# The first batch by input chunks over all outputs, W0 as one tile, and four adds moved: a two-layer fp32 kernel on one core

## The chip, the core and the metric

The kernel runs on one core of a Trainium2 chip. The metric is the device time of one execution in microseconds; for several runs the median is given. A profile is one execution taken by the hardware profiler; its span is the time from the first to the last recorded work on the core.

## What is computed

For each of 8 batches, x is 256 tokens by 1024 features, fp32. In short (the reference's two functions, without the parts that only make inputs):

```python
sign = (2 * mask - 1)                       # mask: (8, 1024, 1024) of int32
x = x + (x @ W0.T + b0 + (x @ sign) * coeff[b])
A, Bm = lora_As[itok], lora_Bs[itok]        # rank 16, one adapter per batch
x = x + (x @ W1.T + b1 + ((x @ A) @ Bm) * 2.0)
```

The first layer has its own weight for every batch: W0 transposed, plus coeff times the sign matrix. So 4 MB of mask have to be read for each batch, and each has to be scaled and added to W0 before TensorE can use it. The second layer has one weight for all.

## The kernel before, in words

Two groups of four batches. In each group, first layer for the four, then second layer for all of them together. All data lie feature-major: partitions are features, tokens are columns.

**First layer, batches 0 to 3** (`first_layer`, L229 to 269). A batch's mask comes in 8 pieces: output half h (0, 1) outermost, input group g (0 to 3) within it; a piece is two input chunks of 128 by 512 outputs, 512 KB. `pieces` (L139) lists them for all batches, and k is a piece's number. For each piece:
- `load(k)` (L161) issues its DMAs on SP's queue: the mask, for batch 0 the matching W0 part (its own tile for each h and g, L167), for h = 0 the x of two input chunks (256 KB). For k below BY_CHUNK = 6 mask and W0 come in two halves, one input chunk each (256 KB); the first x too (128 KB halves). The mask tiles have three buffers.
- `build(k)` (L197) makes the weight: ScalarE's activation (L215) turns the mask into c(2m - 1), VectorE's add (L218) adds W0. In halves where the load was in halves.
- 8 matmuls (L243; a 128x128 weight against 256 tokens) add into two banks of PSUM for the half. Each fp32 matmul stands in the trace as two records of matmul and two of weight load.

Loads run four pieces ahead of the matmuls, builds two ahead. At the end of a half the banks are read: in batches 1 to 3 by ScalarE with the bias (L258); in batch 0 by VectorE with bias and x (L262), because the identity of "x +" isn't in W0 yet. It is added to W0's diagonal blocks (L205, eight adds of 128x128 by VectorE) when piece 8 is built, and is in all later weights.

**Order of work.** Each engine runs its own instructions one after the other, in the order that the framework's scheduler lays down at build time; that can move an instruction ahead of the place where the program wrote it. `tc.issue_after(i)` puts what is written inside it behind instruction i on i's engine. So the reads of batch 0 stand behind the add of the piece two further on (L254), and the sums that prepare the second layer's weights (`combine_weights`) behind the latest build (L833).

**First layer, batches 4 to 7** (`Seven`): each batch as seven products of quarter size with sums of weights and tokens made by VectorE (L295, L311, matmuls L357).

**Second layer** (`second_layer`, L582). The same scheme of seven products on two levels: `plan` (L748) names seven outer products, and `run` (L671) does each as seven inner ones of 8 records (L612). A product's banks are named X, Z and Y; `read` (L661) takes a bank into the output's quarter, by VectorE's add where something is to be added (L664). `add` (L745, one 128x512 add at L746) sums quarters. `beside` is a generator of extra VectorE work, one step of which is written after each of several inner products. The lower-right output quarter c22 gets two such sums, e5 and e1; before the change both are in `last_quarter` (L808), beside the seventh outer product (A22), whose end is `finish` (L723), and the quarter is then stored. `down` and `up` (L640, L621) are the adapter's two small products; `up` also gives c22 its first values, copied by ScalarE (L638) during the fifth outer product.

The kernel's start (L818 to 824): four loads, a one-element activation that makes ScalarE load its table, two builds. c_row, the batch coefficients, is loaded on ScalarE's queue first (L89); TensorE runs idle matmuls meanwhile (L99).

Of the kernel before, what the change touches and what calls it, by code (L numbers as in the profile page):

```python
# [21 lines left out]

# [2 lines left out]
def kernel(  # L25
# [11 lines left out]
    lora_b: bass.AP,  # L37
    outT: bass.AP,
):

# [91 lines left out]
    make_identity(nc, ident)  # L132


    x_sb, m_sb, weff, w0_sb, raw, weff_at = {}, {}, {}, {}, {}, {}
    anchors = {}
    halves_0 = [(h, g) for h in range(2) for g in range(NG)]
    seven_order = [(0, 0), (0, 1), (0, 2), (0, 3), (1, 2), (1, 0), (1, 3), (1, 1)]
    pieces = [(b, h, g) for b in range(B) for h, g in (seven_order if b in SEVEN else halves_0)]  # L139

    def pair(name):
        return qpool.tile([P, 2, CG, OQ], F32, tag="q", name=name)

    def chunks(k: int):

        return [slice(c, c + 1) for c in range(CG)] if k < BY_CHUNK else [slice(0, CG)]

    def chunk(a, c: int):

        flat = a.rearrange("p c f -> (p c f)")  # L150
        return flat.rearrange("(c p f) -> c p f", c=CG, p=P)[c]


    W1_ORDER = [
# [6 lines left out]
    def load(k: int):  # L161


        b, h, g = pieces[k]
        m_sb[k] = mpool.tile([P, CG, OH], I32, tag="m", name=f"m_{k}")
        if b == 0:
            w0_sb[h, g] = const.tile([P, CG, OH], F32, tag=f"w0{h}{g}", name=f"w0_{h}_{g}")  # L167
        if h == 0:
            x_sb[b, g] = xpool.tile([P, CG, T], F32, tag=f"x{g}", name=f"x_{b}_{g}")
        pairs = [(m_sb[k], mask[b, h, g])]  # L170
        if b == 0:
            pairs.append((w0_sb[h, g], w0T[h, g]))
        if h == 0:
            pairs.append((x_sb[b, g], xT[b, g]))
        if k < BY_CHUNK:

            for c in range(CG):
                for i, (t, a) in enumerate(pairs):
                    if i < 2 or k == 0:
                        nc.sync.dma_start(t[:, c], chunk(a, c))  # L180
                    elif c == 0:
                        nc.sync.dma_start(t, a)
        else:
            for t, a in pairs:
                nc.sync.dma_start(t, a)
        if k == NG:
            nc.sync.dma_start(b0_sb, b0)
        if k == 2 * NG:
            nc.sync.dma_start(itok_sb, itok)
        for n, (q, r) in enumerate(W1_ORDER):  # L190
            if k == 0 and r % 2 == 0:
                two = pair(f"w1_{q}_{r // 2}")
                raw[q, r], raw[q, r + 1] = two[:, 0], two[:, 1]
            if k == 2 * NG + 2 + 3 * n // 4:
                nc.sync.dma_start(raw[q, r], w1T[q, r])

    def build(k: int):  # L197

        b, h, g = pieces[k]
        if k == 2 * NG:  # L200

            for c in range(NC):
                j = c % TPH
                d = w0_sb[c // TPH, c // CG][:, c % CG, j * P : (j + 1) * P]
                nc.vector.tensor_add(d, d, ident)  # L205
        if b not in SEVEN or (h == 0 and g < 3):
            pool, tag = wpool, "w"
        elif g >= NG // 2:
            pool, tag = tpool, "T"
        else:  # L210
            pool, tag = qpool, "q"
        w = pool.tile([P, CG, OH], F32, tag=tag, name=f"w_{k}")
        m = m_sb.pop(k)
        for c in chunks(k):
            nc.scalar.activation(  # L215
                w[:, c], m[:, c], AF.Identity, bias=neg_c[:, b : b + 1], scale=two_c[:, b : b + 1]
            )
            weff_at[k] = nc.vector.tensor_add(w[:, c], w[:, c], w0_sb[h, g][:, c])  # L218
            anchors["weights"] = weff_at[k]
        weff[k] = w  # L220

# [4 lines left out]
    def bank(name):  # L226
        return psum.tile([P, 2, T], F32, tag="ps", name=name)

    def first_layer(b: int, h: int, y, beside):  # L229


        ps = [bank(f"ps1_{b}_{h}_{i}") for i in range(TPH // 2)]
        for g in range(NG):
            k = (b * 2 + h) * NG + g
            if k + LOADS_AHEAD < n_pieces:
                load(k + LOADS_AHEAD)
            if k + BUILDS_AHEAD < n_pieces and pieces[k + BUILDS_AHEAD][0] not in SEVEN:
                build(k + BUILDS_AHEAD)
            w = weff.pop(k)
            for c in range(CG):  # L240
                for j in range(TPH):
                    first = g == 0 and c == 0
                    nc.tensor.matmul(  # L243
                        ps[j // 2][:, j % 2, :],
                        lhsT=w[:, c, j * P : (j + 1) * P],
                        rhs=x_sb[b, g][:, c, :],

                        start=first and j % 2 == 0,
                        stop=g == NG - 1 and c == CG - 1,
                        skip_group_check=True,  # L250
                    )
            beside(k)

        with tc.issue_after(weff_at[k + BUILDS_AHEAD].ins) if b == 0 else nullcontext():  # L254
            for j in range(TPH):
                ot = h * TPH + j
                if b > 0:
                    nc.scalar.activation(  # L258
                        y[:, j, :], ps[j // 2][:, j % 2, :], AF.Identity, bias=b0_sb[:, ot : ot + 1]
                    )  # L260
                    continue
                nc.vector.scalar_tensor_tensor(  # L262
                    y[:, j, :],
                    ps[j // 2][:, j % 2, :],
                    b0_sb[:, ot : ot + 1],
                    x_sb[b, ot // CG][:, ot % CG, :],
                    ALU.add,
                    ALU.add,
                )
# [3 lines left out]
    class Seven:  # L273
# [102 lines left out]
        def add(self, i, v, ps):  # L376
            nc.vector.tensor_add(self.out(i, v), ps, self.out(i, v))
# [37 lines left out]
    def behind(what: str):  # L415
        return tc.issue_after(anchors[what].ins) if what in anchors else nullcontext()

    class Sevens:
# [163 lines left out]
    def second_layer(group: int, y, first, first_steps, second):  # L582
# [78 lines left out]
        def read(out, ps, other=None):  # L661
            if other is None:
                return nc.scalar.copy(out, ps)  # L663
            return nc.vector.tensor_add(out, ps, other)  # L664
# [80 lines left out]
        def add(o, x):  # L745
            nc.vector.tensor_add(o, o, x)  # L746
# [91 lines left out]
    for group in range(NGROUP):  # L838
        y = [
            [  # L840
                ypool.tile([P, TPH, T], F32, tag=f"y{i}{h}", name=f"y_{GB * group + i}_{h}")
                for h in range(2)
            ]
            for i in range(GB)
        ]
        first = Right(f"b11_{group}", [y[0][0], y[1][0]])
        second = Right(f"b21_{group}", [y[0][1], y[1][1]])
        first_steps = first.sums()

        def between(b):  # L850
            if b % GB == 2 and group:
                load_adapters(group, y[1][0][:, 0, :1])
            if b % GB == 3:
                next(first_steps)
                next(first_steps)

        sevens[group].run(y, between)
        for i in range(GB):
            if GB * group + i in SEVEN:
                continue  # L860
            between(GB * group + i)
            for h in range(2):
# [12 lines left out]

# [68 lines left out]
```

## Time and profile before

| what | value |
|---|---|
| runs of the kernel, median of 3 | 412.73 us (412.66, 412.73, 423.72) |
| the profiled execution | 411.8 us |
| its span | 410.0 us |
| granted TensorE clock | 0.999 |
| moved by DMA | 97.44 MB, mean 238 GB/s |

Rows of the page's groups and of the timeline read: start and duration (timeline), line, engine, operation, output <- inputs, shape, count, then in brackets the idle time of the engine before it and what ended it. PE is TensorE's matmul, PEld its weight load, DVE is VectorE, ACT ScalarE, POOL GpSimd, SP the queue that issues most loads; a q after a name is the engine's queue of instructions that issue DMAs or wait. In a table of stretches each engine has its busy time and count of instructions, in the order PE, PEld, DVE, ACT, POOL; then come the granted clock, the busy share of the 16 DMA engines and what they moved. A row of DMA issues ends with KB each and the time from issue to landing.

### The profile page before, as it was taken

What the parts mean: (1) busy time and instruction counts of PE and PEld (TensorE: products, weight loads), DVE (VectorE), ACT (ScalarE), POOL (GpSimd) and SP (SyncE); (2) the same over time, 40 slices, a digit from 0 to 9 for tenths busy, and PEclk for the clock granted to TensorE, in tenths of its full rate; (3) what the DMA queues carried; (4) which work ended last, traced back from release to release, by engine and by line L of the source; (5) the groups of instructions that cost most, each with busy time, mean ns of one, the idle gap of its engine ahead of it and who ended that gap; (6) DMA issues with size and microseconds to landing.
All of it is one profiled execution on the core that took longest, in us unless ns stands there. A gap on an engine that the chain in (4) does not pass through costs nothing.

```text
span 410.0 us, 6576 instructions
## 1 busy us (share of the span) xinstructions
PE 403.4 (98%) x2458; PEld 357.4 (87%) x2458; DVE 302.0 (74%) x430; ACT 137.1 (33%) x216; POOL 38.5 (9%) x77
## 2 busy tenths in 40 slices
PE   7999999999999999999999999999999999999996
PEld 5888888888877888877899999999998788888885
DVE  2467597995647658995989999999936365886593
ACT  3544534534344201133115748274221420102200
POOL 0000042566301001000000000400000000000000
PEclk9999999999999999999999999999999999999999
DMA  7999999999997576775895768763022247555662
GB/s 252 388 403 392 296 368 415 412 405 320 413 342 250 139 230 201 217 224 184 235 364 154 258 198 292 221 213 97 26 74 77 77 135 242 165 146 165 194 217 103
DMA packets 42626, 97.44 MB, mean 238 GB/s; under 512 B 5604, under 2 KB 6372, under 8 KB 42596
## 3 DMA queue, kind: packets, MB, share of 16 engines
q1 hardware_dynamic: 33698, 76.30, 56.6%
q0 software_dynamic: 4288, 12.61, 8.1%
q10 hardware_dynamic: 4610, 8.13, 5.2%
q8 instruction: 19, 0.31, 0.3%
q14 instruction: 11, 0.09, 0.1%
HBM read 77.09 MB, written 19.92 MB: 237 GB/s over the span
## 4 chain that ended last, share of the span: by engine, by line
PE 90%; DVE 7%; DMA 1%; issue 1%; ACT 0%; SPq 0%; ACTq 0%; DVEq 0%
PE ps L243 27%; PE X L612 20%; PE X L357 14%; PE Z L612 10%; PE Z L357 7%; PE Y L612 5%; PE Y L357 3%; PE G L629 2%; PE psh L644 2%; DVE e L664 2%; DVE c L746 1%; DMA m<-mask 1%; DVE T L603 1%; DVE c L664 1%; SPq L180 0%
## 5 line engine op out<-in xcount | busy, mean ns | idle before, releaser
L215 ACT ACTIVATE w<-m,neg_c,two_c 128x1024 f32<-128x1024 int32 (+1 forms) x70 | 81.2, 1168 | 106.6 <-DMA m<-mask 44.2
L243 PE MATMUL ps<-x,w 128*128 128x256 f32 x512 | 111.3, 380 | 0.7 <-DVE w L218 0.7
L243 PEld LDWEIGHTS ps<-x,w 128*128 128x128 f32 x512 | 97.2, 190 | 14.9 <-DVE w L218 1.8
L218 DVE TENSOR_TENSOR w<-w,w 128x1024 f32<-128x1024 f32 (+1 forms) x70 | 77.7, 1128 | 32.9 <-ACT w L215 32.9
L746 DVE TENSOR_TENSOR c<-c,e 128x512 f32<-128x512 f32 x48 | 32.0, 686 | 10.1 <-ACT c L638 9.7
L357 PE MATMUL X<-t,s 128*128 128x128 f32 x256 | 29.9, 275 | 0.0
L357 PEld LDWEIGHTS X<-t,s 128*128 128x128 f32 x256 | 29.2, 192 | 0.0
L638 ACT COPY c<-G 128x512 f32<-128x512 f32 x32 | 16.4, 600 | 37.6 <-PE G L629 34.2
L372 ACT ACTIVATE y<-X,b_sb 128x128 f32<-128x128 f32 x48 | 13.6, 365 | 40.0 <-PE X L357 40.0
L664 DVE TENSOR_TENSOR c<-X,c 128x512 f32<-128x512 f32 (+1 forms) x26 | 16.6, 646 | 13.4 <-PE X L612 13.4
L663 ACT COPY e<-X 128x512 f32<-128x512 f32 x16 | 9.4, 588 | 48.0 <-PE X L612 48.0
L612 PE MATMUL X<-T_t,l_S_s 128*128 128x256 f32 x96 | 22.8, 380 | 0.0
L612 PEld LDWEIGHTS X<-T_t,l_S_s 128*128 128x128 f32 x96 | 18.2, 190 | 2.7 <-DVE e L664 0.3
L295 DVE TENSOR_TENSOR s<-w,w 128x1024 f32<-128x1024 f32 x16 | 19.2, 1215 | 0.0
L612 PE MATMUL X<-b_t,l_A_s 128*128 128x256 f32 x64 | 15.5, 386 | 0.0
L357 PE MATMUL Z<-x,s 128*128 128x128 f32 x128 | 15.0, 276 | 0.0
L357 PE MATMUL Y<-x,w 128*128 128x128 f32 x128 | 14.9, 275 | 0.0
L357 PE MATMUL X<-t,w 128*128 128x128 f32 x128 | 14.9, 275 | 0.0
L357 PE MATMUL Z<-t,s 128*128 128x128 f32 x128 | 14.9, 275 | 0.0
L357 PE MATMUL X<-x,w 128*128 128x128 f32 x128 | 14.9, 275 | 0.0
L357 PEld LDWEIGHTS X<-x,w 128*128 128x128 f32 x128 | 14.7, 192 | 0.1
L357 PEld LDWEIGHTS Z<-x,s 128*128 128x128 f32 x128 | 14.6, 192 | 0.0
(123 smaller groups left out, 589.3 us busy)
## 6 DMA issues: line engine op xcount, KB each, us to landing
m<-mask SPq DMA_DIRECT2D x58, 512.0 KB, 6.0
l_S_s<-leaf_S_s SPq DMA_DIRECT2D x32, 256.0 KB, 2.7
x<-xT SPq DMA_DIRECT2D x31, 256.0 KB, 5.4
outT<-c ACTq DMA_DIRECT2D x30, 256.0 KB, 3.5
l_A_s<-leaf_A_s SPq DMA_DIRECT2D x24, 256.0 KB, 3.3
l_S_a<-leaf_S_a SPq DMA_DIRECT2D x24, 256.0 KB, 2.8
w<-w1T SPq DMA_DIRECT2D x16, 256.0 KB, 7.3
leaf_S_s<-S_s POOLq DMA_DIRECT2D x16, 256.0 KB, 7.3
```

Source lines behind the costliest of these rows:

```text
L215: nc.scalar.activation(w[:, c], m[:, c], AF.Identity, bias=neg_c[:, b : b + 1], scale=two_c[:, b : b + 1])
L218: weff_at[k] = nc.vector.tensor_add(w[:, c], w[:, c], w0_sb[h, g][:, c])
L243: nc.tensor.matmul(ps[j // 2][:, j % 2, :], lhsT=w[:, c, j * P : (j + 1) * P], rhs=x_sb[b, g][:, c, :],  start=first and j % 2 == 0, stop= ...
L295: anchors["weights"] = op(s, self.w[x, a], self.w[y, a])
L357: nc.tensor.matmul(ps[:, j, :], lhsT=w[:, c, j * P : (j + 1) * P], rhs=r, start=first and a == 0 and c == 0 and j == 0, stop=False, skip_g ...
L372: nc.scalar.activation(self.out(i, v)[:, j, :], ps[:, j, :], AF.Identity, bias=b0_sb[:, ot : ot + 1])
L612: nc.tensor.matmul(ps[:, j, :], lhsT=l[:, c, j * P : (j + 1) * P], rhs=r[:, c, :], start=first and c == 0 and j == 0, stop=False, skip_gro ...
L629: nc.tensor.matmul(ps[b][:, j, :], lhsT=lb_pad[rows, o : o + P], rhs=h_sb[rows, :], start=j == 0, stop=j == 1, skip_group_check=True,)
L638: nc.scalar.copy(dest[b // 2][u, b % 2], ps[b])
L663: return nc.scalar.copy(out, ps)
L664: return nc.vector.tensor_add(out, ps, other)
L746: nc.vector.tensor_add(o, o, x)
```

## The change

Four things are changed; nothing else is.
- Batch 0 is no longer done half by half. Its piece k is one input chunk (128 rows) over all 1024 outputs: 512 KB of mask, 512 KB of W0. Eight pieces again; x (two chunks) comes with every second one. The eight output blocks add into four banks at once, and all eight reads stand after the eighth piece, behind the add of piece 9. The first three pieces (BY_HALF = 3) are loaded and built in two halves of 512 outputs each.
- The first x chunk is issued on ScalarE's queue instead of SP's.
- W0 is one tile of 128 x 8 x 1024 instead of eight; batches 1 to 7 use the part of it that belongs to their piece. The eight identity adds stand behind the add of piece 7.
- In the second layer the adds of e5 into c22 move from the seventh outer product into the sixth, each behind the latest VectorE read there.

The host lays mask and W0 out to match. The diff, cut to its core:

```diff
-BY_CHUNK = 6
+BY_HALF = 3
...
+    w0_sb = const.tile([P, NC, D], F32, tag="w0", name="w0_sb")
...
+    pieces = [(0, None, c) for c in range(NC)]
+    pieces += [(b, h, g) for b in range(1, B) for h, g in (by_seven if b in SEVEN else by_half)]
...
+    def parts(k: int):
+
+        return [slice(i, i + 1) for i in range(2)] if k < BY_HALF else [slice(0, 2)]
...
+    def w0_of(k: int):
+        b, h, g = pieces[k]
+        if b == 0:
+            return w0_sb[:, g, :].rearrange("p (h o) -> p h o", h=2)
+        return w0_sb[:, g * CG : (g + 1) * CG, h * OH : (h + 1) * OH]
...
+        m_sb[k] = mpool.tile([P, 2, OH], I32, tag="m", name=f"m_{k}")
+        pairs = [(m_sb[k], mask[b, g if b == 0 else h * NG + g])]
         if b == 0:
...
+            pairs.append((w0_of(k), w0T[g]))
+        x_pair = g // CG if b == 0 and g % CG == 0 else g if h == 0 else None
+        if x_pair is not None:
+            x = x_sb[b, x_pair] = xpool.tile([P, CG, T], F32, tag=f"x{x_pair}", name=f"x_{b}_{x_pair}")
+        if k < BY_HALF:
+
+            for i in range(2):
+                for t, a in pairs:
+                    nc.sync.dma_start(t[:, i], part(a, i))
+                if k == 0 and i == 0:
+                    nc.scalar.dma_start(x[:, 0], part(xT[0, 0], 0))
+                elif k == 0:
+                    nc.sync.dma_start(x[:, 1], part(xT[0, 0], 1))
+                elif x_pair is not None and i == 0:
+                    nc.sync.dma_start(x, xT[b, x_pair])
         else:
             for t, a in pairs:
                 nc.sync.dma_start(t, a)
+            if x_pair is not None:
+                nc.sync.dma_start(x, xT[b, x_pair])
...
             for c in range(NC):
-                j = c % TPH
-                d = w0_sb[c // TPH, c // CG][:, c % CG, j * P : (j + 1) * P]
-                nc.vector.tensor_add(d, d, ident)
+                d = w0_sb[:, c, c * P : (c + 1) * P]
+                with tc.issue_after(weff_at[k - 1].ins):
+                    nc.vector.tensor_add(d, d, ident)
...
-        for c in chunks(k):
+        for i in parts(k):
             nc.scalar.activation(
-                w[:, c], m[:, c], AF.Identity, bias=neg_c[:, b : b + 1], scale=two_c[:, b : b + 1]
+                w[:, i], m[:, i], AF.Identity, bias=neg_c[:, b : b + 1], scale=two_c[:, b : b + 1]
             )
-            weff_at[k] = nc.vector.tensor_add(w[:, c], w[:, c], w0_sb[h, g][:, c])
+            weff_at[k] = nc.vector.tensor_add(w[:, i], w[:, i], w0_of(k)[:, i])
...
+    def first_batch(y, beside):
+
+        ps = [bank(f"ps1_0_{i}") for i in range(NC // 2)]
+        for c in range(NC):
+            load(c + LOADS_AHEAD)
+            build(c + BUILDS_AHEAD)
+            w = weff.pop(c)
+            for ot in range(NC):
+                h, j = divmod(ot, TPH)
+                nc.tensor.matmul(
+                    ps[ot // 2][:, ot % 2, :],
+                    lhsT=w[:, h, j * P : (j + 1) * P],
+                    rhs=x_sb[0, c // CG][:, c % CG, :],
+                    start=c == 0 and ot % 2 == 0,
+                    stop=c == NC - 1,
+                    skip_group_check=True,
+                )
+            beside(c)
+
+        with tc.issue_after(weff_at[NC - 1 + BUILDS_AHEAD].ins):
+            for ot in range(NC):
+                h, j = divmod(ot, TPH)
                 nc.vector.scalar_tensor_tensor(
...
-            return nc.vector.tensor_add(out, ps, other)
+            anchors["reads"] = nc.vector.tensor_add(out, ps, other)
+            return anchors["reads"]
...
-        run(5, "S3", right["S3"], e1, e1, then=lambda uv: add(c21[uv], e1[uv]))
+
+        def add_e5():
+
+            for uv in UV:
+                with behind("reads"):
+                    add(c22[uv], e5[uv])
+                yield
+
+        run(5, "S3", right["S3"], e1, e1, beside=add_e5(), then=lambda uv: add(c21[uv], e1[uv]))
 
         def last_quarter():
             for u, v in UV:
-                add(c22[u, v], e5[u, v])
                 add(c22[u, v], e1[u, v])
                 store(c22[u, v], 1, 1, u, v)
                 yield
```

More of the change, by code (lines that the diff above doesn't have):

```diff
@@ L132, with part @@
     make_identity(nc, ident)
-    x_sb, m_sb, weff, w0_sb, raw, weff_at = {}, {}, {}, {}, {}, {}
+    x_sb, m_sb, weff, raw, weff_at = {}, {}, {}, {}, {}
     anchors = {}
-    halves_0 = [(h, g) for h in range(2) for g in range(NG)]
-    seven_order = [(0, 0), (0, 1), (0, 2), (0, 3), (1, 2), (1, 0), (1, 3), (1, 1)]
-    pieces = [(b, h, g) for b in range(B) for h, g in (seven_order if b in SEVEN else halves_0)]
+    w0_sb = const.tile([P, NC, D], F32, tag="w0", name="w0_sb")
+    by_half = [(h, g) for h in range(2) for g in range(NG)]
+    by_seven = [(0, 0), (0, 1), (0, 2), (0, 3), (1, 2), (1, 0), (1, 3), (1, 1)]
+    pieces = [(0, None, c) for c in range(NC)]
+    pieces += [(b, h, g) for b in range(1, B) for h, g in (by_seven if b in SEVEN else by_half)]
     def pair(name):
         return qpool.tile([P, 2, CG, OQ], F32, tag="q", name=name)
[L144 to L151, printed above, removed]
+    def parts(k: int):
+        return [slice(i, i + 1) for i in range(2)] if k < BY_HALF else [slice(0, 2)]
+    def part(a, i: int):
+        flat = a.rearrange("p i f -> (p i f)")
+        return flat.rearrange("(i p f) -> i p f", i=2, p=P)[i]
+    def w0_of(k: int):
[3 more added lines that the diff above has]
+        return w0_sb[:, g * CG : (g + 1) * CG, h * OH : (h + 1) * OH]
     W1_ORDER = [
@@ L164, in load @@
         b, h, g = pieces[k]
-        m_sb[k] = mpool.tile([P, CG, OH], I32, tag="m", name=f"m_{k}")
+        m_sb[k] = mpool.tile([P, 2, OH], I32, tag="m", name=f"m_{k}")
+        pairs = [(m_sb[k], mask[b, g if b == 0 else h * NG + g])]
         if b == 0:
[L167 to L182, printed above, removed]
+            pairs.append((w0_of(k), w0T[g]))
[12 more added lines that the diff above has]
+                    nc.sync.dma_start(x, xT[b, x_pair])
         else:
@@ L252, in first_layer @@
             beside(k)
[L254 to L261, printed above, removed]
+        for j in range(TPH):
+            ot = h * TPH + j
+            nc.scalar.activation(
+                y[:, j, :], ps[j // 2][:, j % 2, :], AF.Identity, bias=b0_sb[:, ot : ot + 1]
+            )
[14 more added lines that the diff above has]
+                    skip_group_check=True,
+                )
+            beside(c)
+        with tc.issue_after(weff_at[NC - 1 + BUILDS_AHEAD].ins):
+            for ot in range(NC):
+                h, j = divmod(ot, TPH)
                 nc.vector.scalar_tensor_tensor(
-                    y[:, j, :],
-                    ps[j // 2][:, j % 2, :],
+                    y[h][:, j, :],
+                    ps[ot // 2][:, ot % 2, :],
                     b0_sb[:, ot : ot + 1],
-                    x_sb[b, ot // CG][:, ot % CG, :],
+                    x_sb[0, ot // CG][:, ot % CG, :],
                     ALU.add,
@@ L861 @@
             between(GB * group + i)
+            if group == 0 and i == 0:
+                first_batch(y[0], step)
+                continue
             for h in range(2):
@@ L903, in pieces @@
         a = a.reshape(*lead, NG, CG, P, D // OH, OH)
-        return laid(a.transpose(*range(n), n + 3, n, n + 2, n + 1, n + 4))
+        a = a.transpose(*range(n), n + 3, n, n + 2, n + 1, n + 4)
+        return laid(a).reshape(*lead, -1, P, CG, OH)
     As = np.asarray(L1_cond_lora_As)
@@ L912 @@
         "mask": pieces(np.asarray(mask_Bx4096x4096_ik1)),
-        "w0T": pieces(np.asarray(L0_cond_W).T),
+        "w0T": laid(np.asarray(L0_cond_W).T.reshape(D // P, P, 2, OH)),
         "b0": laid(np.asarray(L0_cond_b).reshape(D // P, P).T),
@@ L923, with by_part @@
     }
-    def by_chunk(a):
-        a[:] = np.moveaxis(a, -2, -3).reshape(a.shape)
-    for k in range(BY_CHUNK):
-        by_chunk(arrays["mask"][0, k // NG, k % NG])
-        by_chunk(arrays["w0T"][k // NG, k % NG])
-    by_chunk(arrays["xT"][0, 0])
+    def by_part(a):
+        a[:] = np.moveaxis(a, 1, 0).reshape(a.shape)
+    arrays["mask"][0] = np.asarray(mask_Bx4096x4096_ik1)[0].reshape(D // P, P, 2, OH)
+    for k in range(BY_HALF):
+        by_part(arrays["mask"][0, k])
+        by_part(arrays["w0T"][k])
+    by_part(arrays["xT"][0, 0])
     nc = bacc.Bacc("TRN2", target_bir_lowering=False, num_devices=1)
```

## The prediction

> **What bounds the kernel now.** I read the engine shares first, then the chain that ended last.
>
> ```profile
> span 410.0 us, 6576 instructions
> PE 403.4 (98%) x2458; PEld 357.4 (87%) x2458; DVE 302.0 (74%) x430; ACT 137.1 (33%) x216; POOL 38.5 (9%) x77
> PE 90%; DVE 7%; DMA 1%; issue 1%; ACT 0%; SPq 0%; ACTq 0%; DVEq 0%
> ```
>
> TensorE is the bound nearly everywhere. A change that leaves the matmuls alone can only win what TensorE loses at its start, at its end, or in a hole. The chain in order of time, its first and longest pieces:
>
> ```profile
> 2.25 4.70 DMA m<-mask
> 6.98 0.82 ACT w L215
> 7.82 0.70 DVE w L218
> 8.57 109.26 PE ps L243 x504
> ```
>
> From 8.57 to 117.83 us TensorE works through the first layer of group 0. Elsewhere the chain has 24 records of the same kind (L612) in 5.18 us, 0.216 us each; 504 x 0.216 = 108.9, so only 0.4 us of 109.26 is idle. What stands ahead of 8.57 is the second half of piece 0: its mask was issued at 2.25 us and landed 4.7 us later. The timeline shows the holes:
>
> ```profile
> 5.71 1.76 PEld L243 LDWEIGHTS ps<-x,w 128*128 128x128 f32 x8 [0.39 <-DVE w L218]
> 8.57 3.32 PEld L243 LDWEIGHTS ps<-x,w 128*128 128x128 f32 x16 [1.10 <-DVE w L218]
> 12.23 27.92 PEld L243 LDWEIGHTS ps<-x,w 128*128 128x128 f32 x130 [0.34 <-DVE w L218]
> ```
>
> One step (half a piece, 4 matmuls, 8 records) is 1.73 us of TensorE. Step 0 starts at 5.8, step 1 at 8.57, step 3 waits 0.2 to 0.3 more, and then nothing visible. So the most that a better start could give is TensorE running gapless from about 5.5: 5.5 + 64 x 1.73 = 116.2 against 117.83, **1.6 us**. At the end:
>
> ```profile
> 396.87 1.29 DVE L746 TENSOR_TENSOR c<-c,e 128x512 f32<-128x512 f32 x2
> 404.37 1.89 PE L612 MATMUL X<-T_t,l_A_a 128*128 128x256 f32 x8
> 406.30 0.76 DVE L664 TENSOR_TENSOR c<-X,c 128x256 f32<-128x256 f32 x2 [1.04 <-PE X L612]
> ```
>
> The last of the adds at L746 is over at 398.2 us, 8 us before the last matmul; the tail (two half reads and their stores, 3.7 us) has none in it.
>
> What feeds the start is the DMA, in these stretches (DMA share and GB/s are the last two columns):
>
> ```profile
> 3.00:3.50 0.50, 0.50 (x2) 0.47 (x3) 0.24 (x2) 0.00 (x0) 0.00 (x0) 1.00 1.05 401
> 4.00:4.50 0.50, 0.50 (x2) 0.38 (x2) 0.00 (x0) 0.50 (x1) 0.00 (x0) 1.00 0.38 117
> 4.50:5.00 0.50, 0.50 (x3) 0.35 (x2) 0.44 (x1) 0.03 (x1) 0.00 (x0) 1.00 0.97 215
> 10.00:11.00 1.00, 1.00 (x6) 0.89 (x5) 0.76 (x4) 0.36 (x1) 0.00 (x0) 1.00 1.04 399
> ```
>
> A trough at 4 us, where the 128 KB half of the first x passes (third in SP's queue), and from 10 us on about 390 GB/s until 40 us. In batch 0 TensorE and the DMA run level.
>
> **Part 1: batch 0 by single input chunks.** Matmul count and shapes stay: 64 matmuls of two records. What changes is the bytes each stretch of TensorE needs. Before, each of the first four pieces (3.46 us of TensorE) needs mask 512 KB, W0 512 KB, x 256 KB, 1280 KB in all; the last four need 1024 KB. After, each needs 1152 KB on the mean. The sum, 9216 KB, is the same. I place landings on a line drawn through the trace: m of step 3 (2304 KB in the queue's order) landed at 10.6, m of step 11 (6912 KB) at 22.9, where its activation stopped waiting: 375 KB per us.
>
> Steps 0 and 1. x's first half goes to ScalarE's queue right behind c_row (issue ends 1.39), 0.4 us earlier than on SP, and is now the second thing in flight. Today it is what step 0 waits for: issued 1.78, landed 3.8 later at 5.58, while w was ready at 5.25. Step 0 can start at 5.3 to 5.5. Price on ScalarE: one issue of 0.43 us ahead of the table load (1.42 to 1.85, ending at 3.1) and the warm-up activation (to 3.3); the first real one waits for its mask until 3.67, which hides it with 0.35 us to spare. The next mask half moves up from fourth to third in SP's queue: issued at 1.78 instead of 2.25.
>
> Here the Trainium skill speaks against a gain: "DMA: Bandwidth & Descriptors", section "Issuing engines are not separate DMA queues", says that all issuers share the same 16 DMA engines and that a second issuer saves only the sequencer's issue time. By that rule the mask half comes 0.47 us earlier (one issue slot of SP) and the queue behind it not at all. The row says that around 4 us the DMA engines stood at a share of 0.38, so there was room and a filled trough is worth more: at 390 GB/s instead of 117 and 215, 0.4 MB in that one microsecond against 0.17, some 0.6 us. I take 0.35 us for everything behind (between nothing and 0.6, since x itself still has to pass), and 0.5 for the mask half: landed 6.45, activation 0.81, add 0.69, hand-over 0.1: step 1 at about 8.0 instead of 8.57. Step 2 (m at 1536 KB, landed 8.57 today, less 0.35) is ready at 9.8; it started at 10.3. So far 0.5 us won.
>
> An earlier step 0 also meets a TensorE that is still slow: the six idle loads from 3.11 us take 2.21 us, 0.4 us from one to the next, those after 6.2 us 0.215. So its first loads run at half the rate and it gains less than its 0.3 us. That counts for nothing in the sum, since step 1 waits for its own data. Steps 3 to 5 (masks at 2048, 2560 and 3328 KB, less 0.35, and 1.6 us of activation, add and hand-over) are ready at 11.2, 12.5 and 14.6, wanted at 11.5, 13.3 and 15.0: no hole.
>
> **Piece 3, where it is given back.** Halves end after piece 2 (BY_HALF = 3), which is step 5; before, they went on to step 11. Piece 3 is now one mask and one W0 load of 512 KB, one activation of 1.24 us and one add of 1.23, and none of its 8 matmuls starts before all of it. In SP's order its mask ends at 4096 KB and its W0 at 4608 KB: by the line 15.4 and 16.7, less 0.35: 15.0 and 16.4. The activation is over at 16.3; the add runs 16.4 to 17.6; step 6 starts at **17.7**. TensorE would want it at 9.8 + 4 x 1.73 = 16.7, so a new hole of 1.0 us opens. Before, the same step started at 8.57 + 5 x 1.73 + 0.2 = 17.4; counted back from 117.83, 58 steps of 1.727 give 17.65 with the later small gaps in it. The net is 0 to +0.3; I take **+0.1 us**.
>
> How sure is the landing? The nearest rows are the first and the second whole piece of the kernel before, pieces 6 and 7. Piece 6 landed on the line (24.9). Piece 7 did not:
>
> ```profile
> m<-mask SPq DMA_DIRECT2D x1, 512.0 KB, 7.5
> 28.57 1.24 ACT L215 ACTIVATE w<-m,neg_c,two_c 128x1024 f32<-128x1024 int32 x1 [2.40 <-DMA m<-mask]
> ```
>
> Issued at 20.94, landed at 28.45, where the line has 27.6: 0.8 late. Piece 3 is a first whole piece, so I take none of the 0.8, but keep it for the range. Then pieces 4 and 5: W0 at 5632 and 6912 KB, 19.1 and 22.5, ready at 20.4 and 23.8, wanted at 21.2 and 24.6: slack 0.8, gone if they are 0.8 late. x of pieces 2, 4 and 6 (3072, 5888, 8192 KB) lands 1 to 2 us ahead of need. SP itself: the mask of piece 3 needs the buffer of piece 0, free when step 1's activation ends (about 7.3); everything behind waits in SP with it, but over 1.5 MB is then still in flight, 4 us of work.
>
> **W0 as one tile; VectorE at the end of batch 0.** For the later batches the operand becomes two rows of 512 apart in one tile; the trace has no add of that form with one strided operand, the nearest is the plain one, 1.23 us; between 0 and 10% more would be 0.1 us on an engine with slack, so 0. The eight identity adds (0.28 us each, L205), until now scattered from 10 to 31 us, now stand together behind the add of piece 7 (over at 31): 2.0 us, and behind them the add of piece 8: over at 34.4, wanted at 35.0. The eight reads of the banks (four took 1.66 us, so 3.3) stand together behind the add of piece 9: 35.6 to 38.9, and behind them the add of piece 10 ends at 40.1 where TensorE wants it at 41.9. Both hidden, with 0.6 and 1.8 us left: 0.
>
> **The e5 adds.** Four adds of 0.69 us per group move from the seventh product into the sixth, behind its reads. TensorE does not wait for VectorE from 383 us on, nor in group 0 from 188 to 212, and the total is the same: 0 us, with under 0.3 us either way if a read shifts by one add.
>
> **Sum.** +0.1 us at step 6, 0 elsewhere: span 410.1, the profiled execution 411.8 becomes 411.9; the runs' median stands 0.9 above that execution, so **412.8 us**.
>
> **Rivals.**
> A. Forecast: start won, piece 3 gives it back, 412.2 to 413.4. For it: both terms come out of rows. Chance 0.50.
> B. Faster: the filled trough brings forward the whole queue by 0.6 us or more and the 4 KB rows of whole pieces run at the 404 to 412 GB/s seen from 22 to 28 us: W0 of piece 3 at 15.9, step 6 at 17.1, 0.6 less than A; at most the 1.6 us above. About 411.8. Against: the line has no such slack elsewhere. Chance 0.23.
> C. Slower: the second and later whole loads lag as piece 7 did. Place: step 6 to step 10; price: 0.8 us in W0 of piece 3 puts step 6 at 18.5, 413.6; with piece 5 late too, 414.2. It decides from a W0 landing after 16.6. Chance 0.23.
> D. The one tile is taken as one thing: an add then waits for every W0 load already issued. Four pieces ahead are 4.5 MB, 11 us: 424. Against: mask tiles are already loaded in two halves, and the first activation ran at 3.71 while the second half landed at 6.95. Chance 0.03; 0.01 is left for gains nobody sees.
>
> The range 411.3 to 414.5 leaves out D and the edges of B and C, under 0.2. 2% is 8.3 us, about what these runs (412.66 to 423.72) can tell from no change; only D reaches it: faster 0.01, same 0.96, slower 0.03.
>
> **What would show it.** Right: step 1 near 8.0; a hole of about 1 us before the matmuls of piece 3, ended by the add at L218; the first L612 matmul at 117.9 plus or minus 0.6; the tail still 3.7. Wrong: no trough at 4 us but step 1 unchanged (part 1), no hole at piece 3 (B), holes at pieces 4 and 5 (C), a wait of TensorE on VectorE at 35 or 42 us.

## The result, and the profile after

The changed kernel takes **410.92 us** (median of 11 runs, 410.14 to 412.68); the kernel before, on the same chip, 412.73 (11 runs, 411.66 to 423.72; the one of 423.72 is a slow run, which the ratio leaves out). The ratio is 0.9954, with a 95% interval of 0.9934 to 0.9974: within 2%, and still faster, by 1.1 to 2.7 us. The prediction said 412.8, in 411.3 to 414.5: the time lies below that range. The profiled execution took 410.92 us too, with a span of 409.1 instead of 410.0.

The page's shares of the engines, and the shares of the chain that ended last:

```profile
span 409.1 us, 6555 instructions
PE 403.8 (99%) x2458; PEld 358.2 (88%) x2458; DVE 300.7 (74%) x427; ACT 136.0 (33%) x213; POOL 38.6 (9%) x77
PE 91%; DMA 5%; ACT 2%; SPq 1%; DVE 0%; issue 0%; DVEq 0%; ACTq 0%
```

The matmuls are the same 2458 records. What differs is what TensorE lost between them, and the chain hints at where: before, VectorE held 7% of it, now 0%; the DMA held 1% and now 5%. Something on VectorE left the critical path, and transfers of masks took its place, at the start and again from 267 to 277 us.

**The start.** The chain's first pieces (start, length, what):

```profile
3.20 4.59 DMA m<-mask
8.57 5.90 DMA m<-mask
17.13 17.53 PE ps L280 x80
34.66 83.13 PE ps L255 x384
```

Its timeline over the same stretch (start, busy time, engine, line, and in brackets the idle time ahead and what ended it):

```profile
5.50 11.06 PEld L280 LDWEIGHTS ps<-x,w 128*128 128x128 f32 x48 [0.18 <-DVE w L230]
15.85 1.23 DVE L230 TENSOR_TENSOR w<-w,w_sb 128x1024 f32<-128x1024 f32 x1 [1.77 <-ACT w L227]
17.13 17.13 PEld L280 LDWEIGHTS ps<-x,w 128*128 128x128 f32 x80 [0.57 <-DVE w L230]
```

And two of the half-microsecond stretches (the last two columns are the DMA share and GB/s):

```profile
4.00:4.50 0.50, 0.50 (x2) 0.38 (x2) 0.00 (x0) 0.50 (x1) 0.00 (x0) 1.00 1.02 252
4.50:5.00 0.50, 0.50 (x3) 0.35 (x2) 0.25 (x1) 0.13 (x1) 0.00 (x0) 1.00 0.97 295
```

The trough at 4 us is filled (117 GB/s before, 252 now). The second mask half had landed by 6.07 us, step 1's operand was ready at 7.60, and from 5.5 to 16.6 us there is no pause of TensorE worth a line. Then comes the new hole ahead of piece 3: its add starts at 15.85 and TensorE idles 0.57 us until 17.13. Batch 0 ends at 34.66 (34.70 before, counted back from 117.83 by the same 83.13), the first layer of group 0 at 117.80 (117.83 before). So in this execution the whole of part 1 came to **0.03 us**. TensorE's waits from 16.5 to 117 us (sum, count, longest) say where the rest went, first of the changed kernel:

```profile
PEld ps L280 <- DVE w L230: 0.6, 1, 0.6
PEld ps L255 <- DVE w L230: 0.4, 1, 0.4
```

The second one, at 90 us, is for the weight made from the first mask of batch 3. From 9 to 117 us the kernel before had one wait in all:

```profile
PEld ps L243 <- DVE w L218: 0.3, 1, 0.3
```

**Where the 0.9 us of span is.** Down to 182 us the two traces run side by side, 0.03 apart. Then they part, in the fifth of the outer products of group 0. The kernel before, its timeline there (a stretch that the prediction did not show):

```profile
181.41 2.05 ACT L638 COPY c<-G 128x512 f32<-128x512 f32 x4 [3.31 <-DVE c L664]
182.38 1.89 PE L612 MATMUL X<-T,l_S_a 128*128 128x256 f32 x8
183.00 1.29 DVE L746 TENSOR_TENSOR c<-c,e 128x512 f32<-128x512 f32 x2 [0.95 <-ACT c L638]
184.21 0.69 DVE L664 TENSOR_TENSOR c<-X,c 128x512 f32<-128x512 f32 x1
184.95 1.99 PE L612 MATMUL X<-b_t,l_S_a 128*128 128x256 f32 x8 [0.68 <-DVE c L664]
```

The third line holds two e5 adds. The program writes them in the seventh product; the scheduler had placed them here, in the fifth, ahead of a read of bank X. VectorE takes its instructions in order: it idled 0.95 us until ScalarE had copied from G what they add to, added for 1.29 us, and only then read the bank. TensorE's next X product adds into that bank, so it has to wait for the read: it stood idle for 0.68 us in the matmul record (1.08 us in its load), and the bracket names the read, [<-DVE c L664]. The same stretch of the changed kernel:

```profile
181.37 2.05 ACT L669 COPY c<-G 128x512 f32<-128x512 f32 x4 [3.31 <-DVE c L695]
182.55 0.69 DVE L695 TENSOR_TENSOR c<-X,c 128x512 f32<-128x512 f32 x1 [0.53 <-PE X L643]
184.07 1.89 PE L643 MATMUL X<-b_t,l_S_a 128*128 128x256 f32 x8
184.96 0.68 DVE L778 TENSOR_TENSOR c<-c,e 128x512 f32<-128x512 f32 x1
```

The read comes first, at 182.55 instead of 184.21, the product starts without a wait, and the add at L778 goes in later, where nobody waits for it. What follows (the second run of G matmuls) begins at 185.97 instead of 186.95: 0.98 us, of which 0.03 is the start's. The same place in group 1 gives 0.22. The chain has it, first of the kernel before, then of the changed one:

```profile
375.22 5.60 PE X L612 x24
374.68 5.38 PE X L643 x24
```

The books: 0.03 at the start, 0.95 and 0.22 here, and 0.45 lost between 265 and 284 us, where TensorE waited twice, 0.2 us each, for ScalarE's reads, which stood behind activations of late masks of batches 4 to 7: 0.75 of the 0.9. The tail is as long as it was but for 0.1 us (405.55, the start of the last half reads, to 409.1; before, 406.30 to 410.0). The waits at that place come and go with the execution: there are none in the trace of the kernel before, 0.2 us of them in e5_alone, 1.1 in half8 and 1.4 in after_light, three of the runs below.

### The profile page after: what moved, and what is told of

It is laid out like the page before. It is cut to its first block, busy times and chain, and to the rows that moved or that the text cites. A ratio compares the mean times of both kernels' runs of the same rounds, so it can differ in the third digit from the quotient of the medians.

```text
span 409.1 us, 6555 instructions
## 1 busy us (share of the span) xinstructions
PE 403.8 (99%) x2458; PEld 358.2 (88%) x2458; DVE 300.7 (74%) x427; ACT 136.0 (33%) x213; POOL 38.6 (9%) x77
## 4 chain that ended last, share of the span: by engine, by line
PE 91%; DMA 5%; ACT 2%; SPq 1%; DVE 0%; issue 0%; DVEq 0%; ACTq 0%
PE X L643 24%; PE ps L255 20%; PE X L388 12%; PE Z L643 12%; PE Z L388 6%; PE Y L643 6%; DMA m<-mask 5%; PE ps L280 4%; PE Y L388 3%; PE G L660 2%; PE psh L675 2%; ACT w L227 1%; ACT y L403 0%; SPq L186 0%; DVE w L230 0%
## 5 line engine op out<-in xcount | busy, mean ns | idle before, releaser
L227 ACT ACTIVATE w<-m,neg_c,two_c 128x1024 f32<-128x1024 int32 (+1 forms) x67 | 80.1, 1203 | 109.9 <-DMA m<-mask 40.7
L230 DVE TENSOR_TENSOR w<-w,w_sb 128x1024 f32<-128x1024 f32 (+1 forms) x67 | 77.4, 1172 | 36.9 <-ACT w L227 32.7
L778 DVE TENSOR_TENSOR c<-c,e 128x512 f32<-128x512 f32 x48 | 32.0, 683 | 3.9 <-ACT c L669 3.8
L669 ACT COPY c<-G 128x512 f32<-128x512 f32 x32 | 16.4, 600 | 36.4 <-PE G L660 33.1
L695 DVE TENSOR_TENSOR e<-X,e 128x512 f32<-128x512 f32 x16 | 10.9, 684 | 6.6 <-PE X L643 6.6
```

The costliest lines, as they stand in the source:

```text
L227: nc.scalar.activation(w[:, i], m[:, i], AF.Identity, bias=neg_c[:, b : b + 1], scale=two_c[:, b : b + 1])
L230: weff_at[k] = nc.vector.tensor_add(w[:, i], w[:, i], w0_of(k)[:, i])
L669: nc.scalar.copy(dest[b // 2][u, b % 2], ps[b])
L695: anchors["reads"] = nc.vector.tensor_add(out, ps, other)
```

## The experiments

Two theories stood at first. **Order**: the gain is the e5 edit, because it takes two waiting adds from the head of VectorE's queue. **Start**: the gain is batch 0, and its 0.03 us in one trace is chance. All kernels were timed in five rounds beside the kernel before; its medians were 412.97, 413.14 and 413.2 us in the three sets below.

### Each half of the change alone

e5_alone is the kernel before with these edits only:

```diff
-            return nc.vector.tensor_add(out, ps, other)
+            anchors["reads"] = nc.vector.tensor_add(out, ps, other)
+            return anchors["reads"]
...
-        run(5, "S3", right["S3"], e1, e1, then=lambda uv: add(c21[uv], e1[uv]))
+        def add_e5():
+            for uv in UV:
+                with behind("reads"):
+                    add(c22[uv], e5[uv])
+                yield
+        run(5, "S3", right["S3"], e1, e1, beside=add_e5(), then=lambda uv: add(c21[uv], e1[uv]))
...
-                add(c22[u, v], e5[u, v])
                 add(c22[u, v], e1[u, v])
```

> The kernel before with the e5 adds moved into the sixth product behind its reads; batch 0 as it was. Theory 'order' (two e5 adds that the scheduler had put ahead of a bank read in the fifth product wait there for ScalarE's copies, and TensorE waits for the read): the hole at 184 us in group 0 (1.0 us) and the small one in group 1 (0.2) go, 412.7 becomes 411.4 to 411.7, a ratio near 0.997. Rival 'start' (batch 0's new order brings the gain): nothing, 412.5 to 412.9.

Measured: 411.35 us (8 runs), ratio 0.9960 [0.9940, 0.9979]. The hole is gone from its timeline:

```profile
182.64 0.69 DVE L664 TENSOR_TENSOR c<-X,c 128x512 f32<-128x512 f32 x1 [0.53 <-PE X L612]
```

batch0_alone is the changed kernel with exactly these edits undone; the other three changes stay.

> The changed kernel with the e5 adds back in the seventh product, where they were: batch 0's new order, W0 as one tile and x on ScalarE's queue are all that is left of the change. Theory 'order': the hole at 184 us is back; TensorE is done with the first layer 0.0 to 0.1 us earlier than before; 412.4 to 412.8. Rival 'start': 411.0 to 411.4, most of the change's gain, without the e5 part.

Measured: 412.67 us (14 runs), ratio 0.9992 [0.9978, 1.0007]. The hole is back, and as large:

```profile
184.09 1.30 DVE L777 TENSOR_TENSOR c<-c,e 128x512 f32<-128x512 f32 x2 [0.95 <-ACT c L669]
185.30 0.68 DVE L695 TENSOR_TENSOR c<-X,c 128x512 f32<-128x512 f32 x1
186.04 1.99 PE L643 MATMUL X<-b_t,l_S_a 128*128 128x256 f32 x8 [0.69 <-DVE c L695]
```

What follows: the e5 edit alone brings 1.6 us (0.9 to 2.5), batch 0 alone 0.3 us, between 0.9 faster and 0.3 slower. **Start** falls as the main cause. The traces account for 1.0 + 0.2 of the 1.6; the rest lies within the interval and no line shows it.

### Order, or the load of the fifth product?

Moving the adds out of the fifth product also takes 1.3 us of work from it. A rival to **order** is then **load**: VectorE has too much to do there, wherever the adds stand. e5_fifth is the kernel before with all four e5 adds written at the fifth product: two inside it and two at its end, each pinned behind the read that is the latest at that point (`read` keeps its anchor as in e5_alone):

```diff
+        def add_e5(uvs):
+            for uv in uvs:
+                with behind("reads"):
+                    add(c22[uv], e5[uv])
...
             late=lambda: up(1, 1, upper),
+            then=lambda uv: add_e5(UV[:2]) if uv == (1, 1) else None,
         )
+        add_e5(UV[2:])
...
-                add(c22[u, v], e5[u, v])
```

> The kernel before with the e5 adds written into the fifth product itself, two of them pinned behind its second-last reads, two behind its last. Theory 'order': it matters only that they don't stand ahead of the read that TensorE waits for, so the gain is that of the adds in the sixth product within 0.3 us: 411.4 to 411.8. Rival 'load' (the fifth product has more VectorE work than it can hide, and the gain comes from taking the adds out of it): 412.5 to 413.2, no gain.

Measured: 411.37 us (22 runs), ratio 0.9960 [0.9947, 0.9973], as in e5_alone. Its timeline has the first two adds in the fifth product, with their 1.28 us, and the product of TensorE starts without a wait:

```profile
183.68 0.69 DVE L664 TENSOR_TENSOR c<-X,c 128x512 f32<-128x512 f32 x1 [0.53 <-PE X L612]
185.21 1.89 PE L612 MATMUL X<-b_t,l_S_a 128*128 128x256 f32 x8
185.49 1.28 DVE L747 TENSOR_TENSOR c<-c,e 128x512 f32<-128x512 f32 x2
```

**Load** falls. The adds may stand in that product; they may not stand ahead of the read.

### The hole at piece 3

half8 is the changed kernel with all eight pieces of batch 0 in halves, so that no whole piece comes at all in it:

```diff
-BY_HALF = 3
+BY_HALF = 8
```

> The changed kernel with all eight pieces of batch 0 loaded and built in halves (BY_HALF = 8). The prediction's hole ahead of piece 3, 0.6 us in the trace after, should go: step 6 at 16.5 instead of 17.1. If the DMA is not the limit behind it, 0.4 to 0.6 us faster than the change: 410.3 to 410.5. If it is (the pieces behind are wanted as early as they land), no more than 0.1: 410.8 to 411.0.

Measured: 410.35 us (8 runs), ratio 0.9935 [0.9914, 0.9957]; that is in the first of the two ranges, but against the changed kernel's 410.92 the intervals overlap. In its chain, the whole of batch 0 (16 steps of 8 records) is one piece without a hole:

```profile
6.04 28.89 PE ps L280 x128
34.93 82.88 PE ps L255 x384
```

128 records by 0.216 are 27.6 us, yet this took 28.89: in this execution TensorE ran its first loads at half the rate for longer (see the last section), and ended batch 0 at 34.93. So a repeat went with the next set: half8_b, the same kernel; half4, with `BY_HALF = 4`, which makes piece 4 the first whole one; the changed kernel again as after_ctl; and x_on_sp below.

> The changed kernel as it is, beside the next three, so that they can be compared with it and not only with the kernel before. All theories: a ratio of 0.994 to 0.997 to the kernel before.

> All eight pieces of batch 0 in halves, again, beside the changed kernel. Theory 'hole': without the hole ahead of piece 3 it is 0.4 to 1.0 us faster than the changed kernel, where TensorE's slow phase at the start (which ended at 5.3 to 8.3 us in the traces so far) doesn't eat it. Rival 'level': batch 0 ends when the DMA has brought its 9.2 MB, and the times agree within 0.2 us.

> The changed kernel with four pieces in halves (BY_HALF = 4): the whole loads begin at piece 4. Theory 'hole': piece 3 has none any more and piece 4 has a small one (wanted 0.4 us later against its landing than piece 3): between the changed kernel and the one with eight pieces in halves, 0.1 to 0.6 us faster than the changed one. Rival 'level': no difference over 0.2 us.

Measured: after_ctl 410.63 (0.9947 [0.9931, 0.9964]), half8_b 410.25 (0.9939 [0.9921, 0.9957]), half4 410.48 (0.9944 [0.9925, 0.9963]), six runs each. The hole ahead of piece 3 is gone in all three traces that have it in halves (half4 waits 0.2 us for piece 4). In the times it does not show: half8_b is 0.4 us below after_ctl and half4 0.15, with overlapping intervals, so neither the 0.4 to 1.0 that the hole's theory asked for nor the rival's "within 0.2" is decided. One reason is in the traces. Step 6, expected at 16.5, has its first matmul at 17.50 in half8, 17.11 in half8_b and 16.73 in half4, against 17.13 in the changed kernel: in half8 and half8_b TensorE's slow phase at the start took back what the hole gave, and only half4 was 0.4 us ahead.

Another may be further on. Batch 0 ended at 34.54 in half8_b and at 34.21 in half4; but at 90 us these two and after_ctl wait for a weight of batch 3. after_ctl, its waits from 86 to 95 us (sum, count, longest):

```profile
PEld ps L255 <- DVE w L230: 1.0, 1, 1.0
```

and its chain:

```profile
75.39 12.37 DMA m<-mask
90.41 27.89 PE ps L255 x128
```

The first mask of batch 3 is issued at 75.39 and takes 12.4 us to land, among the stores and loads of the second layer's weight sums. The wait is 0.4 us in the first profile of the changed kernel, 0.6 in half8_b and 1.1 in half4, which was also the earliest to end batch 0. (In half8_b the chain there goes through VectorE's weight sums and not through the mask.) That gave a new theory, **level**: what batch 0 wins is given back where the DMA engines set the pace, since they are busy without a break. The changed kernel's stretches there (405 and 415 GB/s, at a DMA share over 1):

```profile
75.00:80.00 5.00, 5.00 (x25) 4.41 (x24) 4.77 (x7) 3.19 (x6) 2.31 (x5) 1.00 1.02 405
80.00:85.00 5.00, 5.00 (x24) 4.39 (x24) 5.00 (x11) 1.24 (x1) 4.04 (x9) 1.00 1.04 415
```

The wait is not bound to the new batch 0, though. e5_fifth, which has the old one, waits there too (timeline):

```profile
88.48 1.24 ACT L215 ACTIVATE w<-m,neg_c,two_c 128x1024 f32<-128x1024 int32 x1 [4.77 <-DMA m<-mask]
91.03 2.02 PEld L243 LDWEIGHTS ps<-x,w 128*128 128x128 f32 x10 [0.42 <-DVE w L218]
```

Of the ten traces with the full writes, seven have this wait; before, e5_alone and half8 don't. In all seven TensorE goes on 2.55 us after that activation starts, anywhere from 87.35 to 88.48, and with it the end of the first layer lies anywhere from 117.80 to 118.93, with either batch 0. What moves the activation by 1.1 us between executions is in no line.

### The level, with the stores taken out

To take load off the DMA there, three kernels store only a scrap of the second layer's weight sums, and every load of a leaf (one such sum) reads one and the same block of W1 instead; the second layer's result is then not the reference's. e5_light is e5_alone with this left out, after_light the changed kernel, half8_light half8:

```diff
-            [P, CG, OQ], F32, tag=f"{outer}{inner}", name=f"leaf_{outer}_{inner}"
+            [P, 1, 64], F32, tag=f"{outer}{inner}", name=f"leaf_{outer}_{inner}"
...
-        nc.gpsimd.dma_start(leaf_at[outer, inner], t)
+        nc.gpsimd.dma_start(leaf_at[outer, inner], t[:, :1, :64])
...
-                anchors["leaves"] = nc.sync.dma_start(t, leaf_at[name, n])
+                anchors["leaves"] = nc.sync.dma_start(t, w1T[0, 0])
```

> Left out: the second layer's weight sums are stored to memory only as a scrap (64 of 512 columns), and every leaf of the second layer is loaded from one block of W1, so that layer's output is not the reference's; the work of the engines is as before. Base of the three: batch 0 as before, e5 adds moved. It takes 11 MB of the writes that fall between 48 and 107 us from the DMA. Theory 'level' (in the full kernels the DMA runs at 405 to 419 GB/s without a break until 90 us, so TensorE waits there for batch 3's first mask whatever it won at the start): no wait at 90 us here; TensorE done with the first layer at 117.8 to 118.2, as with the full writes, since batch 0's holes remain. Rival: no difference in anything.

> The changed kernel with the same left out. Theory 'level': the wait of TensorE at 90 us (0.4 to 1.0 us in the traces of the changed kernel) is gone, and batch 0's gain stays to the end: first layer done at 117.1 to 117.5, 0.4 to 0.8 us before the base of the three, in the medians 0.4 to 0.8 us too. Rival (batch 0's new order gains nothing by itself): within 0.2 us of the base.

> The changed kernel with all eight pieces of batch 0 in halves, the same left out. Theory 'level': with no wait at 90 us the hole ahead of piece 3, which this one doesn't have, counts too: 0.4 to 0.8 us faster than the changed kernel with the same left out, less what TensorE's slow phase at the start takes. Rival: within 0.2 us of it, as with the full writes.

Measured: e5_light 410.87 (0.9932 [0.9906, 0.9958]), after_light 410.39 (0.9929 [0.9902, 0.9956]), half8_light 410.17 (0.9921 [0.9895, 0.9948]). The DMA has room now, as half8_light's stretch shows:

```profile
70.00:80.00 10.00, 10.00 (x48) 8.81 (x47) 9.94 (x17) 5.26 (x7) 6.44 (x13) 1.00 0.85 297
```

and none of the three waits at 90 us. half8_light keeps what it won at the start:

```profile
6.04 27.81 PE ps L280 x128
33.85 82.88 PE ps L255 x384
```

It ends the first layer at 116.73, against 117.75 in e5_light, which has the old batch 0. after_light did not show the gain: its own hole ahead of piece 3 was 1.3 us (step 6 at 17.50), and it ended the layer at 117.92. So the traces speak for a part of **level**: with less to move, the wait is gone, and one start without a hole is kept. But each is one trace, half8_light's slow phase of TensorE also ended early (near 6.1 us, against 8.4 in half8), and the times don't bear it out: after_light was to be 0.4 to 0.8 us below e5_light and is 0.5 by the medians and 0.1 by the ratios; half8_light was to be 0.4 to 0.8 below after_light and is 0.2 to 0.3, with overlapping intervals. **Level** is supported in part, not settled.

### The first x on SP's queue

x_on_sp is the changed kernel with one word other:

```diff
-                    nc.scalar.dma_start(x[:, 0], part(xT[0, 0], 0))
+                    nc.sync.dma_start(x[:, 0], part(xT[0, 0], 0))
```

> The changed kernel with the first x chunk back on SP's queue. Theory of the prediction: the trough of the DMA at 4 us comes back, the second mask half lands 0.4 us later and step 1 starts 0.4 us later; at the end of batch 0 nothing of it is left, since piece 3 waits for its own load: 0.0 to 0.3 us slower than the changed kernel. Rival (the queue for x is what makes batch 0 gain): 0.5 us or more slower.

Measured: 411.58 us (22 runs), ratio 0.9965 [0.9955, 0.9975], beside after_ctl's 410.63 (0.9947): 0.7 us slower by the ratios, 0.95 by the medians, with intervals that overlap at the edge. The timeline of x_on_sp at the second mask half, and the stretch at 4 us:

```profile
6.50 0.81 ACT L227 ACTIVATE w<-m,neg_c,two_c 128x512 f32<-128x512 int32 x1 [2.14 <-DMA m<-mask]
4.00:4.50 0.50, 0.50 (x2) 0.38 (x2) 0.10 (x1) 0.36 (x1) 0.00 (x0) 1.00 0.89 162
```

and of after_ctl:

```profile
5.97 0.81 ACT L227 ACTIVATE w<-m,neg_c,two_c 128x512 f32<-128x512 int32 x1 [1.49 <-DMA m<-mask]
4.00:4.50 0.50, 0.50 (x2) 0.38 (x2) 0.00 (x0) 0.49 (x1) 0.00 (x0) 1.00 1.05 363
```

On SP's queue the trough comes back (162 GB/s against 363) and the mask half comes 0.53 us later; one issue slot of SP is 0.47. The direction holds beyond this pair: the activation of that mask half starts at 5.52 to 6.35 us in the eight traces with x on ScalarE's queue and at 6.41 to 7.26 in the five with x on SP's, but the size of the step depends on the pair. Piece 3's matmuls start at 17.52 in x_on_sp, which is inside the 17.07 to 17.83 of the four traces with the same batch 0 and x on ScalarE's queue, so nothing is shown there. The prediction's theory asked for 0.0 to 0.3 us of total time, its rival for 0.5 or more: the measured 0.7 to 0.95 is on the rival's side. No trace shows where that much comes from, and it stays open.

## Why the prediction was wrong, step by step

**"The e5 adds": the step that failed.** It put them at 0 us, "under 0.3 us either way", since TensorE waits for VectorE neither from 188 to 212 us nor from 383 on. Those are the places where the program *writes* the adds. The scheduler had put two of them elsewhere, at 183 us, and there TensorE did wait. The runs give 1.6 us for this step (e5_alone), and the chain of the kernel before, read at that place, would have shown it (start, length, what):

```profile
181.89 1.09 ACT c L638 x2
183.00 1.29 DVE c L746 x2
184.29 0.61 DVE c L664
184.95 1.99 PE X L612 x8
```

A copy on ScalarE, two adds, a read, and then the matmul: whatever takes the 1.29 us out of that chain shortens it, by up to the idle time of TensorE behind it. The page hinted at it in one number too: VectorE held 7% of the chain, some 29 us, and the prediction accounted for a piece of 0.7 us at the start and never asked where the rest lay. (It lay from 155 to 185 us, ahead of this matmul. That is where to look, not what there is to win: TensorE was idle for about 1 us of it.)

**"Steps 0 and 1": right, with one term missed.** The half x on ScalarE's queue filled the trough. The operands of steps 1 and 2 were ready at 7.60 and 9.35 us, earlier than the predicted 8.0 and 9.8, as the second mask half had landed by 6.07 and not at 6.45. Yet TensorE took step 1 only at 7.95, near the predicted 8.0, because it was still busy with step 0 (timeline, cut at 7.9 us):

```profile
5.50 2.42 PEld L280 LDWEIGHTS ps<-x,w 128*128 128x128 f32 x8 [0.18 <-DVE w L230]
7.95 8.61 PEld L280 LDWEIGHTS ps<-x,w 128*128 128x128 f32 x40
```

The slow first loads, which the sum left out "since step 1 waits for its own data", decided here; in batch0_alone, where they ended earlier, step 1 started at 7.66 with its operand. The agreement with 8.0 is chance. Nor is the room that was read from the DMA share of 0.38 at 4 us a property of the kernel: e5_alone, with the same start, moved 82 GB/s in that half microsecond at a share of 1.15. The trace had been weighed against the Trainium skill's page "DMA: Bandwidth & Descriptors", section "Issuing engines are not separate DMA queues", which grants a second issuer the sequencer's issue time and no more. Between x_on_sp and after_ctl the rule is about right (0.53 against a slot of 0.47); between the kernel before and the changed one the mask came 0.9 us earlier, but there the order of the other loads changed as well.

**"Piece 3, where it is given back": right, and its size varies.** The hole was there, ended by the add as said (L230 in the changed kernel). In the first trace it was 0.57 us instead of 1.0 and step 6 started at 17.13 instead of 17.7. The mask had landed at 14.47 and not 15.0, and W0 before 15.82 and not at 16.4, so the add started at 15.85, when the activation was done, and did not wait for W0. Other executions of the same batch 0 have holes of 0.50 (after_ctl), 1.3 (after_light) and 1.3 (batch0_alone, step 6 at 17.83): the predicted 1.0 lies among them.

**The sum for batch 0**, +0.1 us: the runs give -0.3 with an interval that holds both 0 and +0.1. The predicted end of the first layer, 117.9 give or take 0.6, came at 117.80. Yet step 6 came at 17.13, and 58 steps of 1.727 us from there, as the prediction counts them, end at 117.30: 0.5 us were lost on the way. 0.4 of them is the wait at 90 us for batch 3's mask; the other 0.1 is in no line. The sum had no such wait: it counted what an earlier TensorE needs in batch 0, and not what it meets in the batches behind. That first layer and prediction agree within 0.1 us is luck: the ten traces with the full writes spread over 1.1.

**"W0 as one tile", the identity adds and the reads in one go: right.** The eight identity adds took 1.70 us from 30.21 on, the eight reads 3.22 us from 34.72 on, and TensorE waits for neither. The tail was 3.6 (3.7 predicted).

**Rivals.** C (whole loads lag) did not come; D (one tile taken as one thing) neither. B named the right sign and, for the first trace, step 6 (17.1), but for a gain that the total hardly kept: the 1.6 us came from the edit that no rival was about.

The fastest version by its median, of those that leave nothing out, is half8 with 410.35 and 410.25 us in two sets; from the changed kernel's 410.92 and 410.63 it can't be told apart.

## What to carry to other kernels

Look up a moved instruction where the trace has it and not where the source writes it: an add that waits for another engine, placed ahead of a read that TensorE needs, delays that read by its wait and its own length, and TensorE pays what its slack doesn't cover (1 us here), though VectorE as a whole is idle a quarter of the time. Account for every engine's share of the critical chain before calling an edit on that engine free. And a gain at the start may last only to the next wait further on, such as the one at 90 us here; compare the ends of stages in several traces before counting on it.

## What the runs showed of the hardware

TensorE's slow phase at the start ends at a different time in each execution. Loads that come 0.4 us apart turn into loads 0.215 apart at about 5.3 us in batch0_alone, 6.2 in the kernel before, 6.9 in the changed kernel and 8.4 in half8, though the first matmuls (idle ones) begin at 1.44 us in all and the record of the granted clock says 1.00 throughout. half8, from 6 us on (start, busy time, and the number of loads behind the x):

```profile
5.83 2.79 PEld L280 LDWEIGHTS ps<-x,w 128*128 128x128 f32 x7
```

and batch0_alone:

```profile
7.66 2.03 PEld L280 LDWEIGHTS ps<-x,w 128*128 128x128 f32 x10 [0.70 <-DVE w L230]
```

Seven loads in 2.79 us there (0.43 us from one to the next), ten in 2.03 here. The Trainium skill's page "TensorE: Matmul & The Clock Gate", section "What you observe", has the turn around 4 us into sustained matmul activity, give or take half a microsecond. Counted from 1.44 us, the turns here come after 3.9 to 7.0 us: batch0_alone agrees, the others are later, and the spread is 3 us. For a start that is bound by TensorE and not by its masks, this is up to 1.5 us of scatter between executions (3.1 us at half the rate), nearly as large as the whole effect of the change: the reason why half8's trace, without a hole, still ended batch 0 at 34.93.
